# Group-normalised causal attention: key sums by VectorE transposes instead of a TensorE product, and x normalised by ScalarE

## The chip, the cores and the metric

The kernel runs on one core of one Trainium2 chip. The core has five engines that run their own instruction streams: TensorE (PE, matrix products into PSUM), VectorE (DVE), ScalarE (ACT), GpSimd (POOL) and SyncE (SP, which here issues most DMAs). They wait for one another through semaphores. The metric is the time of one execution on the device in microseconds; the times given are medians of several executions.

## The reference, cut to what matters

```
x = x + attention(group_norm(x))          # x: 32 x 256 x 32 x 32, float32

group_norm: 32 groups of 8 channels; (g - mean) / sqrt(var + 1e-5)
xf = normalised x as B x 256 x 1024
q = q_w xf + q_b;   k, v = kv_w xf + kv_b          # 8 heads of 32 channels
scores = q k^T / sqrt(32)                          # 1024 x 1024 per head
mask   = strictly lower triangle                   # a query sees earlier keys only
attn   = softmax(where(mask, scores, -10000)), then 0 where masked
out    = attn v
```

For each batch element: a group normalisation, three projections of 256 x 256, and for each of 8 heads a strictly causal attention over 1024 positions. The softmax needs, for every query, the sum of its exponentials over all keys: the key sum of this document.

## The kernel before

**Layout.** A batch element is x as two tiles of 128 channels by 1024 positions. Four heads of 32 channels share a tile (a channel group `g`), and the 1024 queries are two halves `hf` of 512. Scores are computed transposed: keys lie on the 128 partitions, queries on the free axis. An exponential tile `e` is 128 keys x 4 heads x 512 queries. No maximum is subtracted; the kernel checks at the end that all key sums lay in a safe range and otherwise runs a second path, `shifted()`, which these inputs do not take.

**Visits.** The work of a batch element is cut into N = 12 visits (`visits` and `products`, lines 515 to 526). In visit i, PE makes the scores of one whole tile `e` and one half tile `eh` (`scores`, product at L276), then a part of a projection (`product`, L168), then the value products of the visit before (`values`, L354). ACT turns scores into exponentials (L332 for `e`, two instructions, and L330 for `eh`), POOL zeroes what lies above the diagonal (L290), and DVE adds the tiles of one (group, half) together (L359), so that one tile of 128 x 4 x 512 partial sums is left: `total`, which lives in an `e0` buffer. There are three pairs of PSUM banks for scores, so that the scores of a visit need the exponentials of the visit before to be done. There are three `e`, four `eh` and four `e0` buffers.

**Order.** PE, ACT, DVE and POOL run in the order in which the program text emits instructions (`manual_schedule`). SP's order is found by a scheduler. Two tables say in which visit a piece of work is emitted: `at` (after the visit's scores, ahead of its value products) and `after` (behind its value products). `PROJECT`, `PREPARE`, `SUMS` and `FINISH` (lines 547 to 551) hold the visits, relative to the first visit of the batch.

**Key sums.** For all but the last two batches, each of the four `total` tiles of a batch is folded by two DMAs that add partitions to partitions (`fold`, L372, issued by POOL): from 128 to 64, then to 32 rows. `stack` (L378) copies the 32 rows into a quarter of the tile `folded` (128 partitions: 4 pairs (group, half) x 32 rows, and 4 heads x 512 queries). There is one `folded` buffer. `sum_folded` then sums the 32 rows of each quarter on PE with a matrix of ones in the right places (`pick_half`), four products of 512 columns into the PSUM bank `misc`, and ACT copies the result (`den`, L385) to SBUF. Through two small transfers by way of DRAM (`sums`, then `rows`) the 8192 sums of the batch are spread over 128 partitions x 64. DVE checks their range (L442, L443) and inverts them (L448), the inverses go to DRAM (L450) and come back, repeated over the 32 channels of their head, as four tiles `rb` (L453). `finish` (L466, L467) multiplies the attention output `num` by them and adds the value bias and x. The last two batches (`late`) use `sums` instead, with products by `pick`.

**Normalising.** `norm_channels` takes mean and variance of each channel (L178, L179), `norm_mean` and `norm_variance` average them over 8 channels with small products on PE and copy the results by ACT (L186, L202), `norm_rstd` raises to -0.5 on POOL (L206), and `norm_apply` (L213, DVE) writes the normalised `xn` in four pieces of 128 x 512, one call for each half of the positions. The projections of the next batch begin in visit 7 of the present one and read `xn`.

**The PSUM bank `misc`.** One bank serves the projections, the small products of the norm and the key sum. In visit 6 of each batch, in which the key sum stands at the end, `scores` is given the projection as `between`: ACT's exponentials come in the order first half of `e`, `eh`, second half of `e`, with the projection's copy ahead of the last one.

Of the kernel before, what the change touches and what calls it, by code (L numbers as in the profile page):

```python
# [17 lines left out]
P = 128  # L18
# [13 lines left out]
def tile_norm_attention_residual(  # L32
# [42 lines left out]
    nc.gpsimd.memset(pick, 1.0)  # L75

    pick_half = const.tile([P, 4, CPG], F32, name="pick_half")
    nc.gpsimd.memset(pick_half, 1.0)
    nc.gpsimd.affine_select(
        out=pick_half, in_=pick_half, pattern=[[-HD, 4], [0, CPG]],  # L80
        compare_op=ALU.is_ge, fill=0.0, base=0, channel_multiplier=1,
    )
    nc.gpsimd.affine_select(
        out=pick_half, in_=pick_half, pattern=[[HD, 4], [0, CPG]],
        compare_op=ALU.is_ge, fill=0.0, base=HD - 1, channel_multiplier=-1,
    )
    pick_half = pick_half.rearrange("p a b -> p (a b)")

# [20 lines left out]
    def unshifted():  # L109
# [71 lines left out]
        def norm_mean(b):  # L181
            mv = live["mv", b]
            pm = misc(f"pm_{b}")
            product(pm[:, :NG], avg, mv[:, :, 0])
            mean = small.tile([P, NG], F32, tag="mean", name=f"mean_{b}")
            nc.scalar.copy(mean, pm[:, :NG])  # L186
            live["mean", b] = mean

        def norm_deviation(b):
            mv, mean = live["mv", b], live["mean", b]  # L190

            dev = small.tile([P, NG], F32, tag="dev", name=f"dev_{b}")
            nc.vector.tensor_sub(dev, mv[:, :, 0], mean)
            nc.vector.tensor_mul(dev, dev, dev)
            nc.vector.tensor_add(dev, dev, mv[:, :, 1])
            live["dev", b] = dev
# [8 lines left out]
        def norm_rstd(b):  # L205
            nc.gpsimd.tensor_tensor(live["rstd", b], live["rstd", b], power, ALU.pow)  # L206

        def norm_apply(b, cols):
            if cols.start == 0:
                live["xn", b] = work.tile([P, NG, S], F32, tag="xn", name=f"xn_{b}")  # L210
            mean, rstd = live["mean", b], live["rstd", b]
            for g in range(NG):
                nc.vector.tensor_scalar(  # L213
                    live["xn", b][:, g, cols], live["x", b][:, g, cols],
                    mean[:, g : g + 1], rstd[:, g : g + 1], ALU.subtract, ALU.mult,
                )

# [78 lines left out]

        def scores(b, full, half, between=()):


# [21 lines left out]
            for j in range(2):  # L321
                lo = scores_of((b, half), short[:, j, 0, :], j)
                for ins in first:
                    tc.declare_no_dep(lo.ins, ins.ins, reason="the semaphore orders them")
            for a in (0, 2, 1) if between else (0, 1, 2):
                if a == 1:
                    for f in between:
                        f()
                if a == 2:
                    exp = nc.scalar.activation(eh.rearrange("p (n bank) q -> p bank n q", n=2), short, AF.Exp)  # L330
                else:
                    nc.scalar.activation(e[:, 2 * a : 2 * a + 2, :], pairs[a], AF.Exp)  # L332
# [33 lines left out]


        def fold(b, n, rows):
            total = live["sum", b, *divmod(n, NH)]
            if (n, rows) == (1, HD):  # L370
                nc.gpsimd.drain()
            nc.gpsimd.dma_start(out=total[:rows], in_=total[rows : 2 * rows], accum_op=ALU.add)  # L372
# [6 lines left out]

        def sum_folded(b):  # L380

            pd = misc(f"pd_{b}")
            sum_keys(pd, live.pop(("folded", b)), slice(0, HALF), slice(0, HALF), of_rows=pick_half)
            den = small.tile([P, HALF], F32, tag="den", name=f"den_{b}")
            nc.scalar.copy(den, pd)  # L385
            live["sums", b] = dram.tile([4, 4, HALF], F32, tag="sums", name=f"sums_{b}")
            nc.sync.dma_start(out=live["sums", b].rearrange("j n c -> (j n) c"), in_=den[::CPG, :])

        def sum_keys(pd, e, cols, of, start=True, stop=True, of_rows=pick):
            for j in range(4):  # L390
                nc.tensor.matmul(  # L391
                    pd[HD * j : HD * (j + 1), of], lhsT=of_rows, rhs=e[:, j, cols],
                    start=start, stop=stop, skip_group_check=True,
                )
# [50 lines left out]
        def invert(b, ns):  # L445
            part = slice(ns.start * HD, ns.stop * HD)
            inv = small.tile([P, ROW], F32, tag="inv", name=f"inv_{b}_{ns.start}")
            nc.vector.reciprocal(inv[part], live["rows", b][part])  # L448
            live["inv", b] = dram.tile([4, 4, HALF], F32, tag="inv", name=f"inverses_{b}_{ns.start}")
            nc.sync.dma_start(out=spread_rows(live["inv", b])[part], in_=inv[part])  # L450
            by_half = live["inv", b] if b >= B - 2 else live["inv", b].rearrange("j n c -> n j c")
            for n in ns:
                nc.sync.dma_start(  # L453
                    out=inverses(b, n),
                    in_=by_half[n].unsqueeze(1).broadcast_to([4, HD, HALF]),
                )
# [76 lines left out]
        def prepare(b, whens):  # L533
            both = [slice(hf * HALF, (hf + 1) * HALF) for hf in range(NH)]
            for n, f in zip(whens, (
                lambda: norm_channels(b, 0), lambda: norm_channels(b, 1), lambda: norm_mean(b),
                lambda: norm_deviation(b), lambda: norm_variance(b), lambda: norm_rstd(b),
                lambda: norm_apply(b, both[0]), lambda: norm_apply(b, both[1]),
            )):
                if n is None:  # L540
# [6 lines left out]
        PROJECT = (-5, -4, -3, -2, -1, 0, 1, 2, 3, 4, 5, 6)  # L547
        PREPARE = (-16, -15, -9, -9, -8, -8, -7, -5)
        SUMS = (3, 7, 9, 13)
# [4 lines left out]
        with tc.manual_schedule(engines={ENG.PE, ENG.Activation, ENG.DVE, ENG.Pool}):  # L554
# [19 lines left out]
            for hf in range(NH):  # L574
                norm_apply(0, slice(hf * HALF, (hf + 1) * HALF))
            units = projections(0)
# [5 lines left out]
            if B > 1:  # L582
                prepare(1, (None, None, 0, 1, 2, 3, 3, 3))
            for b in range(B):
# [15 lines left out]
                if not last:  # L600
                    if not late:
                        when(first + N + 6, lambda b=b: sum_folded(b), after)
                    v = first + N + (2 if late else 8)
                    when(v, lambda b=b: gather(b, every))
                    when(v + 2, lambda b=b: check_sums(b, every))
                    when(v + 2, lambda b=b: invert(b, every))
                    for n in every:
# [10 lines left out]
            for i in range(B * N + 1):  # L618
                if i < B * N:

                    between = at.pop(i, ()) if i % N == 6 else ()
                    scores(i // N, *visits[i % N], between)
                for f in at.pop(i, ()):
# [173 lines left out]
```

## Time and profile before

| what | us |
|---|---|
| median of 3 executions (1859.98 to 1860.07) | 1860.05 |
| the profiled execution | 1858.67 |
| its span, first to last instruction | 1856.6 |

| group | count | mean ns | busy us |
|---|---|---|---|
| L332 ACT `e` 128x1024 | 768 | 1022 | 748.0 |
| L330 ACT `eh` 128x1024 | 384 | 1031 | 395.7 |
| L359 DVE adds, four shapes | 762 | | 1153.4 |
| L391 PE key sum of `folded` | 240 | 592 | 31.2 |
| L385 ACT copy `den` | 30 | 586 | 17.6 |
| L213 DVE `xn` 128x512 | 128 | 642 | 76.8 |
| L178 DVE statistics over 128x512 | 128 | 681 | 81.8 |
| L493 DVE reciprocal 128x512 | 1 | 3345 | 3.3 |
| L206 POOL power 128x2 | 32 | 1372 | 43.9 |
| L442, L443, L448 DVE check and inverse | 31 each | 175, 670, 540 | 43.0 |

An engine's busy time is the union of its instructions. PE's matmuls overlap, and each float32 product shows as two instructions, so that four products are eight rows. The profile's chain of waits follows back from the last instruction what released each step. A timeline row has the start, the duration, the engine and line, the operation with its output and inputs, the shape and the count of merged instructions; in square brackets stands how long the engine was idle before, and for whom it waited.

### The profile page before, as it was taken

The numbers are of one execution on the slowest core, as the hardware profiler recorded it, in microseconds if no ns is written. First come the engines' busy times: TensorE is split into PE (matmuls) and PEld (weight loads), VectorE is DVE, ScalarE is ACT, GpSimd is POOL, SyncE is SP. The second block draws the span as 40 slices with busy tenths as digits, with TensorE's granted clock in tenths as the row PEclk, the third lists the DMA queues.
The fourth block names the chain that finished last, engine by engine and source line by source line (L and its number), as shares of the span: only waits on it lengthen the run. The fifth ranks groups of instructions, "written<-read, shape, count | busy, mean of one in ns | idle before, by whom it ended". The sixth has DMA issues, their size and how long they took to land. (4 is left out here: it accounts for less than half of the span.)

```text
span 1856.6 us, 54181 instructions
## 1 busy us (share of the span) xinstructions
PE 1838.8 (99%) x23440; PEld 932.9 (50%) x23440; DVE 1556.5 (84%) x1601; ACT 1414.5 (76%) x1777; POOL 774.5 (42%) x743
## 2 busy tenths in 40 slices
PE   8999999999999999999999999999999999999997
PEld 5454555454554555554545545555455555454543
DVE  4778888888988888888888888888888888888868
ACT  5777777777777777777777777777777777777776
POOL 2543443434434434344344344443443443434314
PEclk9999999999999999999999999999999999999998
DMA  3457665676666676666766666767567666667412
GB/s 120 70 83 144 140 144 114 116 147 139 141 118 127 133 142 140 140 119 122 140 139 143 123 119 131 145 140 145 108 126 145 139 141 114 129 132 141 98 44 89
DMA packets 77517, 233.43 MB, mean 126 GB/s; under 512 B 19808, under 2 KB 20832, under 8 KB 61912
## 3 DMA queue, kind: packets, MB, share of 16 engines
q0 software_dynamic: 15360, 94.39, 36.7%
q1 hardware_dynamic: 61096, 135.51, 24.7%
q8 instruction: 186, 3.05, 0.7%
q14 instruction: 59, 0.48, 0.1%
q10 hardware_dynamic: 816, 0.00, 0.0%
HBM read 68.41 MB, written 35.62 MB: 56 GB/s over the span
## 5 line engine op out<-in xcount | busy, mean ns | idle before, releaser
L332 ACT ACTIVATE e<-sT 128x1024 f32<-128x1024 f32 x768 | 748.0, 1022 | 356.5 <-PE sT L276 302.0
L359 DVE TENSOR_TENSOR e<-e,eh 128x1024 f32<-128x1024 f32 x381 | 524.0, 1389 | 260.4 <-PE acc L354 186.2
L359 DVE TENSOR_TENSOR e<-e,e 128x1536 f32<-128x1536 f32 x381 | 629.4, 1652 | 15.4 <-POOL e L290 1.0
L290 POOL TENSOR_SCALAR_AFFINE_SELECT e<-e 128x512 f32<-128x512 f32 (+1 forms) x256 | 368.3, 1439 | 617.7 <-ACT e L332 595.1
L276 PE MATMUL sT<-q,k 32*128 32x256 f32 (+3 forms) x7168 | 606.3, 458 | 0.8 <-ACT k L230 0.8
L276 PEld LDWEIGHTS sT<-q,k 32*128 32x128 f32 x7168 | 444.1, 184 | 169.9 <-ACT eh L330 65.6
L168 PE MATMUL pp<-xn,wT 128*32 128x512 f32 x4096 | 492.3, 598 | 0.0
L354 PE MATMUL acc<-e,v 128*32 128x512 f32 (+2 forms) x4096 | 400.7, 486 | 0.3 <-POOL e L290 0.3
L330 ACT ACTIVATE eh<-sT 128x1024 f32<-128x1024 f32 x384 | 395.7, 1031 | 0.0
L372 POOL DMA_DIRECT2D e<-e x240 | 199.5, 893 | 400.3 <-PE sT L276 159.7
L168 PE MATMUL ppv<-wT,xn 128*32 128x256 f32 x4096 | 247.3, 382 | 0.0
L354 PEld LDWEIGHTS acc<-e,v 128*32 128x32 f32 x4096 | 132.5, 110 | 223.7 <-issue 200.2
L354 PE MATMUL acc<-eh,v 128*32 128x256 f32 x3072 | 224.4, 379 | 0.0
L168 PEld LDWEIGHTS pp<-xn,wT 128*32 128x32 f32 x4096 | 107.0, 109 | 219.5 <-issue 197.2
L354 PEld LDWEIGHTS acc<-eh,v 128*32 128x32 f32 x3072 | 98.4, 110 | 165.0 <-issue 152.9
L168 PEld LDWEIGHTS ppv<-wT,xn 128*32 128x32 f32 x4096 | 120.2, 109 | 102.5 <-issue 32.1
L290 POOL TENSOR_SCALAR_AFFINE_SELECT eh<-eh 128x512 f32<-128x512 f32 x128 | 165.1, 1289 | 0.1
L230 ACT ACTIVATE k<-pp,qk_bias 128x512 f32<-128x512 f32 x128 | 89.4, 698 | 13.5 <-PE pp L168 12.4
L467 DVE SCALAR_TENSOR_TENSOR rb<-rb,v_bias_col,x 128x512 f32<-128x512 f32 x126 | 95.9, 761 | 4.5
L230 ACT ACTIVATE q<-pp,qk_bias 128x512 f32<-128x512 f32 x128 | 89.9, 702 | 1.9 <-PE pp L168 1.9
L466 DVE TENSOR_TENSOR rb<-num,rb 128x512 f32<-128x512 f32 x126 | 87.8, 696 | 0.1
L178 DVE BATCH_NORM_STATS2 st<-x 128x6 f32<-128x512 f32 x128 | 81.8, 681 | 5.5 <-DMA x<-in_x_dram 5.5
(70 smaller groups left out, 533.1 us busy)
## 6 DMA issues: line engine op xcount, KB each, us to landing
e<-e POOLq DMA_DIRECT2D x120, 512.0 KB, 7.9
x<-in_x_dram SPq DMA_DIRECT2D x64, 512.0 KB
out_dram<-rb SPq DMA_DIRECT2D x127, 256.0 KB
rb<-inverses SPq DMA_DIRECT2D x126, 256.0 KB
e<-e POOLq DMA_DIRECT2D x120, 256.0 KB, 4.6
folded<-e SPq DMA_DIRECT2D x120, 256.0 KB
rows<-sums SPq DMA_DIRECT2D x31, 32.0 KB
inverses<-inv SPq DMA_DIRECT2D x31, 32.0 KB
```

The costliest lines, as they stand in the source:

```text
L168: nc.tensor.matmul(out[part], lhsT=lhsT[:, part], rhs=rhs, start=start, stop=stop, skip_group_check=True)
L178: nc.vector.bn_stats(st[:, c, :], live["x", b][:, g, c * HALF : (c + 1) * HALF])
L230: nc.scalar.activation(live[key][:, cols], pp, AF.Identity, bias=qk_bias[:, n, g : g + 1], scale=(SCALE, 1.0)[n],)
L276: return nc.tensor.matmul(pair[:, cols], lhsT=live["k", b, g][rows, kb * P : (kb + 1) * P], rhs=live["q", b, g][rows, hf * HALF + of.start ...
L290: nc.gpsimd.affine_select(out=diagonal, in_=diagonal, pattern=[[0, 4], [0, n], [1, P]], compare_op=ALU.is_gt, fill=0.0, base=0, channel_mu ...
L330: exp = nc.scalar.activation(eh.rearrange("p (n bank) q -> p bank n q", n=2), short, AF.Exp)
L332: nc.scalar.activation(e[:, 2 * a : 2 * a + 2, :], pairs[a], AF.Exp)
L354: nc.tensor.matmul(acc[HD * j : HD * (j + 1), of], lhsT=live["v", b][:, kb, h * HD : (h + 1) * HD], rhs=e[:, j, cols], start=first, stop=l ...
L359: nc.vector.tensor_add(total[:, :, of], total[:, :, of], e[:, :, cols])
L372: nc.gpsimd.dma_start(out=total[:rows], in_=total[rows : 2 * rows], accum_op=ALU.add)
L466: nc.vector.tensor_mul(rb, num[:, within], rb)
L467: nc.vector.scalar_tensor_tensor(rb, rb, v_bias_col[:, g : g + 1], xt[:, g, cols], ALU.add, ALU.add)
```

## The change

For all but the last two batches, `sum_folded` no longer uses PE. For each of the four heads DVE turns the 128 x 512 slice of `folded` in square blocks of 32 x 32 (`transpose`), so that the 32 rows of a quarter come to lie along the free axis, and adds them up along it (`tensor_reduce`) into 16 columns of `rows`. Two heads are done behind visit 6, two behind visit 7. `rows` is thus filled on the chip, with no copy by ACT and no `sums` and `rows` transfers. Check and inversion move from visit N+10 to N+8. The inverses are turned back by one more transpose of 128 x 64 and written to DRAM by four DMAs, in runs of 32 values. `pick_half` goes. The last two batches keep their way of summing and its visits.

`norm_apply` handles one of four pieces of 128 x 512 per call, behind visits 5, 6, 7 and 8, and is an ACT instruction, rstd * x + shift, with shift = -mean * rstd from a new small product on POOL; batch 0 stays with DVE. ACT writes the mean with its sign turned. `between` goes, and with it the special order of exponentials in visit 6.

```diff
         def norm_mean(b):
...
-            nc.scalar.copy(mean, pm[:, :NG])
-            live["mean", b] = mean
+            nc.scalar.activation(mean, pm[:, :NG], AF.Identity, scale=-1.0)
+            live["minus_mean", b] = mean
...
         def norm_rstd(b):
-            nc.gpsimd.tensor_tensor(live["rstd", b], live["rstd", b], power, ALU.pow)
+            rstd = live["rstd", b]
+            nc.gpsimd.tensor_tensor(rstd, rstd, power, ALU.pow)
+            live["shift", b] = small.tile([P, NG], F32, tag="shift", name=f"shift_{b}")
+            nc.gpsimd.tensor_tensor(live["shift", b], live["minus_mean", b], rstd, ALU.mult)
...
+        def norm_apply(b, hf, g):
...
+            cols = slice(hf * HALF, (hf + 1) * HALF)
+            xn, xt = live["xn", b][:, g, cols], live["x", b][:, g, cols]
+            rstd = live["rstd", b][:, g : g + 1]
+            if b == 0:
+                nc.vector.tensor_scalar(xn, xt, live["minus_mean", b][:, g : g + 1], rstd, ALU.add, ALU.mult)
+            else:
+                nc.scalar.activation(xn, xt, AF.Identity, bias=live["shift", b][:, g : g + 1], scale=rstd)
...
-            for a in (0, 2, 1) if between else (0, 1, 2):
-                if a == 1:
-                    for f in between:
-                        f()
+            for a in range(3):
...
-        def sum_folded(b):
-
-            pd = misc(f"pd_{b}")
-            sum_keys(pd, live.pop(("folded", b)), slice(0, HALF), slice(0, HALF), of_rows=pick_half)
-            den = small.tile([P, HALF], F32, tag="den", name=f"den_{b}")
-            nc.scalar.copy(den, pd)
-            live["sums", b] = dram.tile([4, 4, HALF], F32, tag="sums", name=f"sums_{b}")
-            nc.sync.dma_start(out=live["sums", b].rearrange("j n c -> (j n) c"), in_=den[::CPG, :])
+        def sum_folded(b, heads):
+            if heads.start == 0:
+                live["rows", b] = small.tile([P, ROW], F32, tag="rows", name=f"rows_{b}")
+            for j in heads:
+                turned = small.tile([P, HALF], F32, tag="den", name=f"turned_{b}_{j}")
+                nc.vector.transpose(turned, live["folded", b][:, j, :])
+                nc.vector.tensor_reduce(
+                    live["rows", b][:, j * HALF // HD : (j + 1) * HALF // HD],
+                    turned.rearrange("p (k r) -> p k r", r=HD), AX.X, ALU.add,
+                )
...
-            nc.sync.dma_start(out=spread_rows(live["inv", b])[part], in_=inv[part])
...
+            if b >= B - 2:
+                nc.sync.dma_start(out=spread_rows(live["inv", b])[part], in_=inv[part])
+            else:
+                turned = small.tile([P, ROW], F32, tag="inv_turned", name=f"inv_turned_{b}")
+                nc.vector.transpose(turned, inv)
+                for n in ns:
+                    nc.sync.dma_start(
+                        out=live["inv", b][n].rearrange("(a j) (m c) -> (j m) a c", a=2, c=HD),
+                        in_=turned[n * HD : (n + 1) * HD].rearrange("p (a c) -> p a c", a=2),
+                    )
...
-        PREPARE = (-16, -15, -9, -9, -8, -8, -7, -5)
+        PREPARE = (-16, -15, -9, -9, -8, -8, -7, -6, -5, -4)
...
-                    if not late:
-                        when(first + N + 6, lambda b=b: sum_folded(b), after)
-                    v = first + N + (2 if late else 8)
-                    when(v, lambda b=b: gather(b, every))
-                    when(v + 2, lambda b=b: check_sums(b, every))
-                    when(v + 2, lambda b=b: invert(b, every))
+                    if late:
+                        when(first + N + 2, lambda b=b: gather(b, every))
+                    else:
+                        when(first + N + 6, lambda b=b: sum_folded(b, every[:2]), after)
+                        when(first + N + 7, lambda b=b: sum_folded(b, every[2:]), after)
+                    v = first + N + (4 if late else 8)
+                    when(v, lambda b=b: check_sums(b, every))
+                    when(v, lambda b=b: invert(b, every))
```

## The prediction

> **What bounds the kernel now.** I read the page's first two parts, then the waits of TensorE (PE), then the timeline around one visit in the middle, and last the chain. One batch is twelve visits. Batch 15 is used throughout; its visit 6 begins at 901.11 us of the span.
>
> ```profile
> PE 1838.8 (99%) x23440; PEld 932.9 (50%) x23440; DVE 1556.5 (84%) x1601; ACT 1414.5 (76%) x1777; POOL 774.5 (42%) x743
> PEclk9999999999999999999999999999999999999998
> ```
>
> PE is busy 99% in every slice at a full granted clock. A busy share alone proves little, since the ends of matmuls are modelled, so the starts decide:
>
> ```profile
> 901.11 1.57 PE L276 MATMUL sT<-q,k 32*128 32x256 f32 x16
> ...
> 905.21 0.61 PE L354 MATMUL acc<-eh,v 128*32 128x256 f32 x8
> 905.64 1.04 PE L391 MATMUL pd<-folded,pick_half 128*32 128x512 f32 x8
> 906.62 1.58 PE L276 MATMUL sT<-q,k 32*128 32x256 f32 x24
> ...
> 911.27 1.57 PE L276 MATMUL sT<-q,k 32*128 32x256 f32 x16
> ...
> 929.89 1.57 PE L276 MATMUL sT<-q,k 32*128 32x256 f32 x16
> ...
> 934.54 1.58 PE L276 MATMUL sT<-q,k 32*128 32x256 f32 x24
> ```
>
> The L276 rows are the score products with which a visit begins. Visit 6 lasts 906.62 - 901.11 = 5.51 us. Visit 0 (929.89 to 934.54) has the same tile shapes and lasts 4.65; visit 7, 4.65 as well. The only thing more in visit 6 is the key sum at L391, so that costs PE 0.86 us. In PE's waits all causes add up to about 9 us, at the program's two ends. In the stretch 897.00 to 953.85 (one batch, 56.85 us) PE is busy all 56.85, DVE 48.45 and ACT 43.92. So PE sets the pace, and DVE and ACT have some 8 and 13 us to spare per batch. The chain agrees in the middle; only its last 50 us run over DVE.
>
> **PE: what goes.** L391 with `folded` stands for 240 instructions, 8 a time, so 30 batches. 30 x 0.86 = 25.8 us, if nothing else becomes late. `pick_half`'s setup on POOL (0.24 + 0.22 + 0.12 us) goes too, beside the first load (DVE waits 5.16 us for it): nothing.
>
> **ACT: four applies in, one copy out.** Per batch `den` (0.59) goes and four `xn` of 128x512 come. These are the rows to price one by:
>
> ```profile
> L230 ACT ACTIVATE q<-pp,qk_bias 128x512 f32<-128x512 f32 x128 | 89.9, 702 | 1.9 <-PE pp L168 1.9
> L362 ACT COPY num<-acc 128x512 f32<-128x512 f32 x128 | 76.4, 597 | 8.9 <-PE acc L354 8.9
> ```
>
> L230 carries one per-partition operand (the bias), L362 none. The nearest row alone would say 0.70 us, and the only row out of SBUF (L479, two of them) 0.72. The Trainium skill, "ScalarE: Activation LUTs", section "What ACT_TABLE_LOAD costs", says that each per-partition pointer operand adds about 93 ns and that instructions in a row overlap by as much. The two rows differ by 105 ns, which agrees, and the apply has two pointers (scale and bias): 0.70 + 0.10 = 0.80. By the row four applies are 2.8 us, by the rule 3.2; I take 0.80, or 0.70 net of overlap. ACT becomes 43.92 - 0.59 + 3.2 = 46.5 of 56.0 us. What counts is the place. The applies follow the projection's copy (and `num`, where there is one) and stand ahead of the next visit's first exponential, for which ACT now idles:
>
> ```profile
> 902.29 1.02 ACT L332 ACTIVATE e<-sT 128x1024 f32<-128x1024 f32 x1 [0.94 <-PE sT L276]
> ...
> 906.75 0.59 ACT L385 COPY den<-pd 128x512 f32<-128x512 f32 x1
> 908.09 1.94 ACT L332 ACTIVATE e<-sT 128x1024 f32<-128x1024 f32 x2 [0.75 <-PE sT L276]
> ...
> 912.46 1.94 ACT L332 ACTIVATE e<-sT 128x1024 f32<-128x1024 f32 x2 [0.94 <-PE sT L276]
> ...
> 916.74 1.94 ACT L332 ACTIVATE e<-sT 128x1024 f32<-128x1024 f32 x2 [0.37 <-PE sT L276]
> ```
>
> The number in brackets is idle time. Visits 6 and 8 have 0.94 for 0.70: hidden. In visit 7 the apply takes `den`'s place: `num` still starts 0.14 us into the visit, ends at 0.73, the apply at about 1.43, and the exponential is due at 1.47: hidden with next to nothing over. In visit 9, 0.37 is too little: its exponentials come 0.33 later. There `eh` ends at 919.59, PE wants that bank at 920.57, so 0.98 - 0.33 = 0.65 us is left: still hidden. At the end of visit 7, 0.33 us remain too (`eh` ends at 910.94, products at 911.27). So an apply stalls PE only from about 1.1 us on. The new order of exponentials in visit 6 (whole tile first, `eh` last) lets `eh` end 4.04 us into it, as in visit 0, before 4.65: nothing.
>
> PE also waits for the applies. The first projection from `xn` comes in visit 7 and needs the first two: the second channel group, ready at about 1.43, is read only by the second half of the products (1.51 + 0.86 = 2.37). The next pair, for visit 9, has the same margin of some 0.8 us.
>
> **POOL: one small multiply.** It stands behind the power at L206 (896.93 to 898.37); behind it is a mask at 900.00, for which POOL idled 1.63 us. Its price lies between L295 (0.10) and the power itself (1.44); both fit, and the first apply is not due before 901.25. Taken as 0.3, hidden. Mean by an ACTIVATE with a factor instead of a copy: at most L202 - L186 = 0.10 us, once on the start-up path.
>
> **DVE: four applies out, transposes and sums in.** Out: 4 x 0.642 (L213) = 2.57. In: per batch four transposes T and four reductions R of 128x512, one transpose of 128x64. R: nearest is L178, which also reads 512 columns into a few, 0.68. The Trainium skill, "VectorE: DVE Perf Modes", "Rules for kernel authors", speaks against this: a reduction on a hot path is the slowest vector operation and should be restructured. By that rule the change would give PE's gain back; by the row, four R are 2.7 us on an engine that has 8 to spare, so the rule doesn't decide here. T has no row: not below half of L213's quickest pair (1.00 us at 912.27), 0.5, and not above the dearest DVE row at this size, the reciprocal L493, 3.35. I take 0.70, the price of L178, an operation that passes each element once. Sum: 4 x (0.70 + 0.68) + 0.15 - 2.57 = +3.1, DVE 51.6 of 56.0 us.
>
> The place again: between 903.42 and the add at 919.90 DVE idles twice, 1.94 and 2.79 us = 4.73. There come 5.5 (sums) + 1.55 (checks, reciprocal, transpose, two visits earlier than now) and go 2.42 (applies): +4.6, in a stretch 0.86 shorter. So DVE arrives about 0.8 us late at 919.90, and catches up in visit 10, which no longer has the checks (1.4). Who waits for DVE: exponentials, for a free `e` or `eh`. The nearest is `eh` of visit 11 (928.53), which needs the add that ends at 921.1: 7 us of cover.
>
> **Queues.** SP loses the stores of `sums` and `inverses` and the load of `rows`, and gets four small stores: one issue more per batch (0.3 to 0.5 us). The next batch's first `stack` now waits for DVE's fourth transpose instead of PE's sum; behind it queue only the inverse stores, which need DVE later still. The inversion moves up two visits and past the second `stack`, which then waits behind four stores, their landing (now 70.4 us in 32 waits, 2.2 each) and four broadcasts; that tile is read some 30 us later. The first output is multiplied at 940.11; broadcasts are issued from 928.03 now and then some 6 us earlier: hidden even if stores in 128-byte runs land 2 us slower. The two transfers through DRAM that go were hidden already.
>
> **Sum.** The profiled execution took 1858.67 us around its span of 1856.6. 1858.67 - 25.8 + 0.1 (start) + 0.1 (the last but one batch, where an apply and a `den` copy meet) = 1833.1. The median shown is 1.4 us above the profiled one, so the forecast is **1834.5 us**.
>
> **Rivals.**
> - *ACT becomes late* (chance 0.09). For: visits 7 and 8 end with 0.33 and less to spare. Against: it needs applies of over 1.1 us, or other gaps. At 1.3 us visits 7 and 8 lose some 0.2 each: 30 x 0.4 = 12, so 1846.
> - *DVE becomes the bound, slower than before* (0.05). Mechanism: a transpose of 4-byte elements that runs at a quarter of the rate, like the 128x2048 add of L359 (2.27 us). DVE would need 48.45 - 2.57 + 0.15 + 4 x (2.27 + 0.68) = 57.8 us a batch: 30 x (57.8 - 56.85) = +29, so 1888. It decides from T = 2.0 on. Against: one pass over 512 columns is 0.7.
> - *The 0.86 us turn into another wait* (0.02): the key sum gave ACT time to copy in visit 6, and PE waits for the bank instead. Time 1860. Against: without `den` ACT has less to do there, and the sums above leave a gap.
>
> The forecast has 0.84. Its own range is 1833 to 1837. Half of the ACT case and the small margin in visit 7 extend it to 1841; the low end is 1832.5, since only PE's 25.8 us are there to win. A measurement of this kernel tells about 0.2% (3.7 us) from no change. Faster 0.93 (forecast and ACT case), same 0.02, slower 0.05.
>
> **What would show it.** Visit 6 at 4.65 us from start to start, PE's waits near 9 us, applies at about 0.80 us on ACT, the idle time before the exponentials of visit 9 gone, T + R near 1.4 and DVE near 92%. It is wrong if exponentials wait for DVE's adds, if PE waits for `eh` or `xn`, or if T is over 2 us.

## The result, and the profile after

The median went from 1860.06 us (1859.98 to 1860.38, 4 runs) to 1836.63 us (1836.06 to 1837.18, 4 runs): a ratio of 0.9874, with a 95% interval of 0.9859 to 0.9889. That is 23.4 us less; the forecast was 25.6 less (1834.5). The same two kernels measured later on another chip (`after_again`, below) came to 1861.32 and 1836.78, 24.5 less. The profiled execution of the changed kernel took 1836.99 us, its span 1835.3. The lines below are of this kernel, so their numbers have shifted: scores L269, exponentials L321 and L319, value products L343, adds L348.

The timeline of PE around visit 6 of batch 15 (start, duration, engine and line, operation, tiles, shape, count):

```profile
891.17 1.57 PE L269 MATMUL sT<-q,k 32*128 32x256 f32 x16
892.68 1.92 PE L156 MATMUL pp<-xn,wT 128*32 128x512 f32 x16
894.42 1.05 PE L343 MATMUL acc<-e,v 128*32 128x384 f32 x16
895.28 0.61 PE L343 MATMUL acc<-eh,v 128*32 128x256 f32 x8
895.83 1.58 PE L269 MATMUL sT<-q,k 32*128 32x256 f32 x24
```

The score products of visit 7 follow directly on the last value product: 895.83 - 891.17 = 4.66 us where there were 5.51. The other visits of batch 15 have kept their length to the hundredth (0: 4.65, 2: 4.22, 3: 5.12, 9: 5.08), so this batch takes 55.99 us instead of 56.85. Thirty visits 6 make 30 x 0.86 = 25.8.

The groups that are new, by shape (count, busy us and mean ns of one, then the idle time before them):

```profile
L209 ACT ACTIVATE xn<-x,shift,rstd 128x512 f32<-128x512 f32 x124 | 103.3, 833 | 0.0
...
L375 DVE STREAM_TRANSPOSE turned<-folded 128x512 f32<-128x512 f32 x120 | 84.2, 702 | 0.0
L376 DVE TENSOR_REDUCE rows<-turned 128x16 f32<-128x512 f32 x120 | 82.3, 686 | 4.1
...
L197 POOL TENSOR_TENSOR shift<-mean,rstd 128x2 f32<-128x2 f32 x32 | 22.3, 695 | 2.5
...
L446 DVE STREAM_TRANSPOSE inv_turned<-inv 128x64 f32<-128x64 f32 x30 | 7.4, 245 | 1.0
```

And batch 15 as one stretch (length, then busy us and instructions of PE, weight loads, DVE, ACT and POOL, then the granted clock):

```profile
863.12:919.11 55.99, 55.99 (x725) 28.60 (x722) 51.95 (x56) 46.06 (x59) 25.10 (x25) 1.00 0.67 133
```

PE still fills the batch. DVE has gone from 48.45 to 51.95 us in this batch and ACT from 43.92 to 46.06. Over the page, PE is at 99%, DVE at 90% (84% before) and ACT at 81%.

**Where 2.4 us of the 25.8 stayed.** From the start of the first visit to the start of the last, the profiled execution went from 1819.06 to 1795.08 us: 24.0 less. The rest of the gain is missing in three places, for which the prediction had only 0.1. Visit 3 of two batches is 0.27 and 0.34 us longer, because in visit 2 an exponential waits for the second `stack` of the batch before to free its `e0` buffer. In the last batch but one (visits 8 and 9, counted from the start of batch 30) 1.15 us are missing. Both waits stand in the groups and waits of ACT:

```profile
ACT e L321 <- DMA folded<-e: 16.1, 12, 1.9
```

```profile
L416 ACT COPY den<-pd 128x512 f32<-128x512 f32 x6 | 3.5, 586 | 7.7 <-PE pd L383 5.4 <-DVE rows L376 2.2
```

In the first, the numbers are the sum, the times and the longest in us: twelve waits, nearly all hidden. In the second, one copy of the late way of summing waits 2.2 us for a reduction of the new way: `turned` was put under the tag `den`, which has two buffers, so the two ways share them. This wait is about 1.0 of the 1.15 us: where it is taken away (experiment 7), 0.16 us remain, and `norm_only`, which has the applies on ACT but no `turned`, has 0.19 more in visit 9 as well.

The other differences between the two profiled executions can't be put down to moving the key sum. The first score product of the changed kernel starts at 18.28 us instead of 16.74, and what follows the start of the last visit is 1.1 us longer. But a run with the key sum still on PE (`norm_only`, below) starts its scores at 17.84 us and has the same end of 22 us, and all other profiled runs lie between 17.84 and 19.17: the kernel before was the odd one in its profiled execution, which at 1858.67 lay below its own median. Of the 1.1 us at the end, 0.9 are one short instruction of DVE, which is told in the last section. In these two traces the start goes with the granted clock; the stretches from 11 to 13 us, of before and of after:

```profile
11.00:13.00 2.00, 2.00 (x20) 1.42 (x22) 1.63 (x4) 1.35 (x3) 0.33 (x1) 1.00 1.02 410
```

```profile
11.00:13.00 2.00, 2.00 (x12) 2.00 (x11) 1.67 (x4) 1.39 (x3) 0.49 (x2) 0.50 1.03 414
```

PE was granted its full clock in the first and half in the second, and the same twelve transposes of weights take 1.53 us before and 2.69 after. The cause stays open: in `sums_only` and `turn_reduce_twice` they take 2.82 us, though the profile shows no half clock there.

### The profile page after: what moved, and what is told of

It reads as the page before. It is cut to its first block, busy times and chain, and to the rows that moved or that the text cites. A ratio compares the mean times of both kernels' runs of the same rounds, so it can differ in the third digit from the quotient of the medians.

```text
span 1835.3 us, 53874 instructions
## 1 busy us (share of the span) xinstructions
PE 1815.7 (99%) x23200; PEld 925.6 (50%) x23200; DVE 1650.8 (90%) x1747; ACT 1481.1 (81%) x1871; POOL 797.1 (43%) x772
## 4 chain that ended last, share of the span: by engine, by line
PE 96%; DVE 3%; ACT 1%; issue 0%; DMA 0%; SPq 0%; DVEq 0%; ACTq 0%
PE sT L269 31%; PE acc L343 26%; PE pp L156 25%; PE ppv L156 13%; DVE e L348 1%; DVE rb L493 0%; DVE rb L466 0%; ACT e L321 0%; DMA x<-in_x_dram 0%; DVE rb L467 0%; PE pv L156 0%; ACT eh L319 0%; PE pd L383 0%; PE wt L135 0%; PE pm L156 0%
## 5 line engine op out<-in xcount | busy, mean ns | idle before, releaser
L321 ACT ACTIVATE e<-sT 128x1024 f32<-128x1024 f32 x768 | 745.9, 1025 | 274.6 <-PE sT L269 202.5
L348 DVE TENSOR_TENSOR e<-e,e 128x1536 f32<-128x1536 f32 x381 | 638.8, 1677 | 20.3 <-POOL e L283 2.7
L348 DVE TENSOR_TENSOR e<-e,eh 128x1024 f32<-128x1024 f32 x381 | 523.9, 1389 | 133.6 <-PE acc L343 113.6
L283 POOL TENSOR_SCALAR_AFFINE_SELECT e<-e 128x512 f32<-128x512 f32 (+1 forms) x256 | 379.4, 1482 | 591.6 <-ACT e L321 571.6
L269 PE MATMUL sT<-q,k 32*128 32x256 f32 (+3 forms) x7168 | 607.2, 458 | 0.8 <-ACT k L223 0.8
L269 PEld LDWEIGHTS sT<-q,k 32*128 32x128 f32 x7168 | 443.0, 184 | 158.0 <-ACT eh L319 65.6
L343 PE MATMUL acc<-e,v 128*32 128x512 f32 (+2 forms) x4096 | 400.7, 486 | 0.0
L319 ACT ACTIVATE eh<-sT 128x1024 f32<-128x1024 f32 x384 | 397.6, 1036 | 0.0
L343 PEld LDWEIGHTS acc<-e,v 128*32 128x32 f32 x4096 | 132.5, 110 | 223.4 <-issue 192.1
L343 PE MATMUL acc<-eh,v 128*32 128x256 f32 x3072 | 224.4, 379 | 0.0
L343 PEld LDWEIGHTS acc<-eh,v 128*32 128x32 f32 x3072 | 98.4, 110 | 165.0 <-issue 152.9
L209 ACT ACTIVATE xn<-x,shift,rstd 128x512 f32<-128x512 f32 x124 | 103.3, 833 | 0.0
```

What stands on the lines that cost most here:

```text
L209: nc.scalar.activation(xn, xt, AF.Identity, bias=live["shift", b][:, g : g + 1], scale=rstd)
L269: return nc.tensor.matmul(pair[:, cols], lhsT=live["k", b, g][rows, kb * P : (kb + 1) * P], rhs=live["q", b, g][rows, hf * HALF + of.start ...
L283: nc.gpsimd.affine_select(out=diagonal, in_=diagonal, pattern=[[0, 4], [0, n], [1, P]], compare_op=ALU.is_gt, fill=0.0, base=0, channel_mu ...
L343: nc.tensor.matmul(acc[HD * j : HD * (j + 1), of], lhsT=live["v", b][:, kb, h * HD : (h + 1) * HD], rhs=e[:, j, cols], start=first, stop=l ...
L348: nc.vector.tensor_add(total[:, :, of], total[:, :, of], e[:, :, cols])
```

## The experiments

Averages of visits are over batches 5 to 24. Two theories about the gain stood against each other: that PE's key sum is all of it, and that part of it comes from moving the normalisation. About the limit there were two as well: that DVE has some 4 us a batch to spare, as its busy time says, or that it is nearer to being the bound.

**1. `norm_only`: only the normalisation moves.** The kernel before, with the four applies on ACT, the shift on POOL and the new `PREPARE`; the key sum stays on PE.

```diff
-                nc.vector.tensor_scalar(
-                    live["xn", b][:, g, cols], live["x", b][:, g, cols],
-                    mean[:, g : g + 1], rstd[:, g : g + 1], ALU.subtract, ALU.mult,
-                )
...
+                nc.scalar.activation(xn, xt, AF.Identity, bias=live["shift", b][:, g : g + 1], scale=rstd)
...
-        PREPARE = (-16, -15, -9, -9, -8, -8, -7, -5)
+        PREPARE = (-16, -15, -9, -9, -8, -8, -7, -6, -5, -4)
```

> The kernel before with only the x normalisation moved to ScalarE in four pieces; the key sums stay on PE with their special order in visit 6. Theory (all of the gain is PE's key sum): 1860 (1859 to 1861.5), visit 6 still 5.51 us, VectorE some 2.6 us a batch less busy for nothing. Rival (relief of VectorE is part of the gain): 1850 or less. Rival (the pieces cost time on ScalarE): 1865 or more.

Measured: 1861.47 us against 1860.40 (ratio 1.0007, 0.9998 to 1.0015). The timeline of PE around its visit 6:

```profile
902.20 1.57 PE L281 MATMUL sT<-q,k 32*128 32x256 f32 x16
...
906.73 1.04 PE L396 MATMUL pd<-folded,pick_half 128*32 128x512 f32 x8
907.71 1.58 PE L281 MATMUL sT<-q,k 32*128 32x256 f32 x24
```

The key sum is there and the visit lasts 5.51 us. So moving the normalisation alone gains nothing, and the four applies on ACT cost PE nothing.

**2. `sums_only`: only the key sums move.** The changed kernel, with `norm_apply` back on DVE, two pieces behind visit 5 and two behind visit 7.

```diff
-                nc.scalar.activation(xn, xt, AF.Identity, bias=live["shift", b][:, g : g + 1], scale=rstd)
+            nc.vector.tensor_scalar(xn, xt, live["minus_mean", b][:, g : g + 1], rstd, ALU.add, ALU.mult)
...
-        PREPARE = (-16, -15, -9, -9, -8, -8, -7, -6, -5, -4)
+        PREPARE = (-16, -15, -9, -9, -8, -8, -7, -7, -5, -5)
```

> The key sums by VectorE as in the changed kernel, but x normalised by VectorE as before (two pieces behind visit 5, two behind visit 7; the latter stand behind the transposes and sums of visit 7). Theory (PE sets the pace, and what counts for VectorE is the place of each piece, not its share): VectorE needs about 54.3 of 56.0 us a batch, which would fit, but the second pair of x pieces comes about 2.4 us into visit 9, where PE wants it at 1.5: PE waits about 1 us a batch for it, 30 batches, so about 1866 (1860 to 1870), and PE's waits show VectorE's x pieces. Rival (only the share counts): 1837, no such wait. Rival (VectorE is then the bound outright): well above 1870, with exponentials waiting for VectorE's adds.

Measured: 1874.19 us, slower than before (1.0075, 1.0058 to 1.0092) and above the 1860 to 1870 of the theory: the place of the loss was right, the size too small. Among PE's waits:

```profile
PE pp L156 <- DVE xn L204: 26.1, 28, 1.3
```

Visit 6 is 4.65 us here too, but visit 9 is 6.07 instead of 5.08, where PE waits for `xn`, and visit 3 is 0.31 longer. The gain of visit 6 is given back in other visits of the same batch.

**3. `sums_early`: the same, with all four applies behind visit 5.** It was to take the wait for `xn` away.

```diff
-        PREPARE = (-16, -15, -9, -9, -8, -8, -7, -7, -5, -5)
+        PREPARE = (-16, -15, -9, -9, -8, -8, -7, -7, -7, -7)
```

> As sums_only, but all four x pieces on VectorE stand behind visit 5, ahead of the transposes. Theory (place, not share): the same load on VectorE, x is ready about 5 us into visit 6 and wanted 6.1 us into it, so PE waits for nothing: 1837 to 1840. Rival (VectorE's share of some 97% of a batch is too much wherever it stands): about as slow as sums_only, 1860 and more.

Measured: 1915.27 us (1.0294, 1.0276 to 1.0312): a miss by far. Visit 9 is 5.08 again, as meant, but visit 2 rose from 4.22 to 5.22 and visit 3 from 5.12 to 6.90. The waits of PE and of ACT show the way:

```profile
PE sT L264 <- ACT e L316: 32.1, 50, 2.3
```

```profile
ACT e L316 <- DMA folded<-e: 104.3, 27, 5.4
```

The likely chain: DVE, held up by the applies, finishes the inverses later; their stores and the broadcasts stand on SP ahead of the batch's second `stack`; an `e0` buffer comes free only when that `stack` has read it; ACT wants the buffer in visit 2 of the next batch. Only its last link is in the lines above; experiment 7 tests the queue, in the changed kernel. The wait moved from one visit to two others.

**4. `reduce_twice`, `turn_reduce_twice`: DVE loaded further.** In the changed kernel each reduction is done twice (4 x 0.686 = +2.7 us a batch), then each transpose too (+5.5). The values are the same.

```diff
                 nc.vector.transpose(turned, live["folded", b][:, j, :])
+                nc.vector.transpose(turned, live["folded", b][:, j, :])      (second kernel only)
+                nc.vector.tensor_reduce(
...
                 nc.vector.tensor_reduce(
...
```

> Each sum along rows by VectorE is done twice (the second overwrites the first with the same values): 4 x 0.69 = 2.75 us more a batch on VectorE, 51.95 + 2.75 = 54.7 of 56.0. Theory (VectorE is off the path until about 56 us): within 3 us of the changed kernel, 1837 to 1840. Rival (at 90% busy VectorE is the bound already): 30 x 2.75 = 82 more, about 1919.

> Each transpose and each sum along rows is done twice: 5.55 us more a batch on VectorE, 57.5 against 56.0 us. Theory (VectorE becomes the bound from 56.0 on): 30 x (57.5 - 56.0) = 45 us more and, with the waits that VectorE can't avoid (2.3 us a batch now), up to 110 more: 1880 to 1945, exponentials waiting for VectorE's adds. Rival (some other slack hides it): 1840 or less.

Measured: 1888.53 us (1.0157, 1.0140 to 1.0174) and 1971.88 us (1.0605, 1.0588 to 1.0623). The first is a miss, the second costs more than the top of what was expected. In `reduce_twice` the loss lies in visit 4 (6.48 instead of 4.75), where PE's small product `pv` waits for the three short deviation instructions:

```profile
908.78 0.24 PE L156 MATMUL pv<-dev,avg 128*32 128x2 f32 x8 [1.69 <-DVE dev L183]
```

This is a waiter that the prediction did not name. Two readings were left: that this wait is the one thin spot, or that DVE as a whole has become the bound and `pv` only happens to be the first in line.

**5. `reduce_twice_dev_early`, `reduce_twice_all_mended`: the thin spot taken away.** Both have the doubled reductions. The mean and the deviation are emitted behind visit 1 instead of 3; the second kernel has the repairs of experiment 7 too.

```diff
-        PREPARE = (-16, -15, -9, -9, -8, -8, -7, -6, -5, -4)
+        PREPARE = (-16, -15, -11, -11, -8, -8, -7, -6, -5, -4)
```

> The doubled reductions again (VectorE +2.75 us a batch), but the mean and the three small deviation instructions are emitted behind visit 1 instead of visit 3, so that two visits lie between them and the small product pv that PE makes in visit 4. Theory: the 28 us a batch sum lost with doubled reductions were PE waiting in visit 4 for the deviation, and nothing else; then visit 4 is 4.75 again, PE no longer waits on that line, and the time is 1837 to 1845 (some single visits 3 longer, by the late second stack). Rival: VectorE as a whole is too late and only the next waiter in the order takes the wait over (exponentials of visit 2, visit 3 then 5.5 to 6.5): 1860 to 1889.

> The same, with the broadcasts also moved behind visit 11 and the turned tile in its own buffer. Theory: with both known ways from VectorE to PE opened, VectorE at some 54.7 of 56.0 us a batch costs PE nothing: visits 3 and 4 at 5.12 and 4.75 in all batches, 1835.5 to 1840. Rival: a third waiter, not named yet, keeps the time above 1850.

Measured: 1921.29 us (1.0329, 1.0311 to 1.0346) and 1928.54 us (1.0372, 1.0355 to 1.0390). Visit 4 is 4.93 and PE no longer waits for `dev`, but both times are worse than that of `reduce_twice`, and the first lies above even its rival's 1860 to 1889. The theory of one thin spot falls. New waits have come up. PE's own in the steady batches are for POOL's masks, for its fill of one row and for ACT's copies (18.8, 15.5 and 7.9 us), not for DVE; ACT's in `reduce_twice_dev_early` are:

```profile
ACT num L351 <- DVE rb L470: 48.9, 25, 3.6
ACT e L321 <- DVE e L348: 38.9, 13, 3.1
...
ACT eh L319 <- DVE e L348: 28.5, 26, 1.2
```

They are all waits for DVE: for the outputs, before a `num` buffer comes free, and for the adds, before an `e` or `eh` buffer does. What all these kernels have in common is found by splitting the batch on DVE itself, from the start and end of each of its instructions, averaged over twenty batches (5 to 24). "Waits" are gaps of over 0.15 us, "gaps" the shorter ones between instructions, which stay (some 1.9 us) even where DVE never waits. The three columns add up to the batch.

| kernel | batch us | DVE busy | gaps | waits | busy with L348's adds |
|---|---|---|---|---|---|
| before | 56.85 | 48.79 | 1.38 | 6.67 | 36.55 |
| `norm_only` | 56.85 | 46.69 | 1.58 | 8.57 | 36.54 |
| after | 56.01 | 51.95 | 1.69 | 2.36 | 36.84 |
| `sums_only` | 57.29 | 55.17 | 1.57 | 0.54 | 37.01 |
| `sums_early` | 58.82 | 56.49 | 1.62 | 0.63 | 37.90 |
| `reduce_twice` | 57.80 | 55.91 | 1.88 | 0.00 | 38.04 |
| `reduce_twice_dev_early` | 58.98 | 57.07 | 1.95 | 0.05 | 39.13 |
| `reduce_twice_all_mended` | 59.44 | 57.38 | 2.02 | 0.05 | 39.01 |
| `turn_reduce_twice` | 60.61 | 58.62 | 2.03 | 0.02 | 38.32 |

(The adds are L359 before the change; the line differs by kernel.) The changed kernel leaves DVE 2.36 us a batch, not 4. Doubled reductions ask for 2.75, and then DVE never waits again: it is the bound, and where PE meets it is a matter of the order. The sum closes: busy +3.96, of which 2.75 are the second reductions and 1.20 the adds, which have become longer; idle -2.17; together +1.79, the measured 57.80 - 56.01. Why the adds get longer is told in the last section. Those of `turn_reduce_twice` are 1.48 us a batch longer than in the changed kernel, some 44 us over 30 batches, which its expected range did not have. That moving `dev` made it worse still is explained in part only: the adds grew by another 1.09 us a batch, because they start with more of POOL's masks still to run (last section), but why this order brings that about was not tried.

The table also says more of experiments 2 and 3 than their own waits do. The key sums ask for 4 x (0.702 + 0.686) + 0.245 = 5.8 us, and without the move of the normalisation a batch of 55.99 leaves just 6.67 - 0.86 = 5.8 of waits. Busy time and gaps of `sums_only` come to 56.7 us, those of `sums_early` to 58.1: neither fits into 55.99. The waits for `xn` and for the `e0` buffer are where PE met a DVE that was all but full.

**6. `apply_twice`: ACT loaded further.** Each apply is done twice (+2.9 us of ACT a batch, beside 9.9 idle).

```diff
                 nc.scalar.activation(xn, xt, AF.Identity, bias=live["shift", b][:, g : g + 1], scale=rstd)
+                nc.scalar.activation(xn, xt, AF.Identity, bias=live["shift", b][:, g : g + 1], scale=rstd)
```

> Each x piece on ScalarE is written twice: 4 x 0.73 = 2.9 us more a batch, 46.06 + 2.9 = 49 of 56.0 us. Theory (place counts: an x piece of more than about 1.1 us makes the exponentials of visits 7 and 8 so late that PE waits for the bank): PE loses some 0.35 us at the end of visit 7, 0.5 at visit 8 and 0.2 at visit 9, 31 batches: about 1868 (1855 to 1880), although ScalarE's share is only 88%. Rival (share counts): 1837.

Measured: 1883.51 us (1.0128, 1.0111 to 1.0145); slower, as the theory said, but above its 1855 to 1880, and the places are not those named. Visits 7, 8 and 9 were to lose 0.35, 0.5 and 0.2 us; they take +0.17, +0.00 and +1.34. PE in visit 9:

```profile
925.17 2.21 PE L270 MATMUL sT<-q,k 32*128 32x256 f32 x16
927.31 1.07 PE L156 MATMUL pp<-xn,wT 128*32 128x512 f32 x8
928.87 1.07 PE L156 MATMUL pp<-xn,wT 128*32 128x512 f32 x8 [0.49 <-ACT xn L210]
```

The score products take 2.21 us instead of 1.57, held by the exponentials of visit 8, and the projection waits 0.49 us for the last piece of `xn`. ACT runs from 911.6 to 932 without a wait, four visits in a row, and the lateness adds up; at 83% of the span it is still far from full. So ACT's room is local too: one apply a visit fits, two don't.

**7. `own_buffer`, `late_spread`, `both_mended`: the 1.8 us that were lost.** The first gives `turned` a buffer of its own; the second issues the broadcasts of the inverses behind visit 11, so that the second `stack` stands behind one of them instead of four; the third does both. `after_again` is the changed kernel, for comparison on the same chip.

```diff
-                turned = small.tile([P, HALF], F32, tag="den", name=f"turned_{b}_{j}")
+                turned = small.tile([P, HALF], F32, tag="turned", bufs=1, name=f"turned_{b}_{j}")
...
+            if b >= B - 2:
+                spread(b, ns)
+
+        def spread(b, ns):
             for n in ns:
                 nc.sync.dma_start(
...
+                    if not late:
+                        when(first + N + 11, lambda b=b: spread(b, every), after)
```

> The changed kernel itself, to be compared with the next three on the same chip: about 1836.6 by every theory.

> The changed kernel with one buffer of its own for the turned slices, instead of the two that they share with ScalarE's copies of key sums in the last two batches. Theory (in the last but one batch ScalarE's copy waited 2.18 us for VectorE's sum to free that buffer, and PE lost 1.15 us in visits 8 and 9): 1.2 us less than after_again, that wait gone. Rival (the copy would have waited for PE anyway): no difference.

> The changed kernel with the four broadcasts of the inverses issued behind visit 11, so that the second stack of the next batch stands on the queue behind one broadcast instead of four. Theory (the stack was late because of the broadcasts, and an exponential tile of visit 2 waits for the buffer that it frees): ScalarE's waits for that transfer, 16.1 us in 12 times, go to nearly none, and with them PE's 0.6 us in two batches: 0.6 less than after_again. Rival (the stack waits for the fold ahead of it, not for the broadcasts): the waits stay.

> Both of the last two edits together. Theory: 1.8 us less than after_again, about 1834.8, and 1.3% less than before. Rival: no difference.

| kernel | median us | lowest, highest | start of first to start of last visit |
|---|---|---|---|
| `after_again` | 1836.78 | 1836.12, 1837.22 | 1795.12 |
| `own_buffer` | 1837.01 | 1835.90, 1838.14 | 1794.20 |
| `late_spread` | 1836.35 | 1836.20, 1837.33 | 1794.45 |
| `both_mended` | 1835.39 | 1835.14, 1836.64 | 1793.45 |

In `late_spread` visit 3 is 5.12 in every steady batch, and ACT has no wait for `folded` left. In `own_buffer` and `both_mended` the 2.2 us wait of the `den` copy is gone; in `both_mended` the last batch but one takes 60.07 us instead of 61.06. So both losses are shown by their own waits. The times of the single repairs can't be told from `after_again` (their runs overlap, and `own_buffer`'s median, expected to be 1.2 us lower, is not). Both together are 1.4 us lower at the median, where 1.8 were expected; these runs overlap too, by one of four, and the firmer number is the 1.7 us between the visits in the profiles. `both_mended` is the fastest of all, at a ratio of 0.9865 (0.9849 to 0.9882) to before, an interval that overlaps with the change's.

## Why the prediction was right

**PE.** The step "the only thing more in visit 6 is the key sum at L391, so that costs PE 0.86 us" held to the hundredth, and `norm_only` shows that it is the whole gain. Of the three rivals none came: PE's waits are some 11 us in all, none in the middle of the program, where 9 were named; 1.2 of the difference are at the very end (last section). One reading was too strong: the page's digits show 90% or more of a slice, not 99% in every one, but the forecast rests on the starts of visits.

**ACT.** By the nearest row an apply would take 0.70 us, by what the Trainium skill, "ScalarE: Activation LUTs", section "What ACT_TABLE_LOAD costs", says of pointer operands 0.80; it took 0.83, nearer to the rule. ACT's batch is 46.06 against 46.5: four applies added 46.06 - 43.92 + 0.59 = 2.73, or 0.68 each net of overlap, for which 0.70 stood in the prediction but not in its sum. The timeline of ACT in visits 7 to 9, which begin at 895.83, 900.48 and 904.70:

```profile
896.45 0.81 ACT L209 ACTIVATE xn<-x,shift,rstd 128x512 f32<-128x512 f32 x1
897.30 1.94 ACT L321 ACTIVATE e<-sT 128x1024 f32<-128x1024 f32 x2
...
901.67 1.94 ACT L321 ACTIVATE e<-sT 128x1024 f32<-128x1024 f32 x2 [0.24 <-PE sT L269]
...
905.44 0.85 ACT L209 ACTIVATE xn<-x,shift,rstd 128x512 f32<-128x512 f32 x1
906.15 1.97 ACT L321 ACTIVATE e<-sT 128x1024 f32<-128x1024 f32 x2
```

In visit 7 the apply ends 897.26 - 895.83 = 1.43 us into the visit, as worked out, and the exponential starts at 1.47. In visit 8 there is 0.24 to spare. In visit 9 the idle time is gone and the exponentials start at 1.45 us, some 0.2 late (0.33 was reckoned) and hidden. The point at which it would stall, 1.1 us an apply, was bounded only: 1.65 us in `apply_twice` stalls.

**POOL.** The multiply took 0.70 us, between the ends of 0.10 and 1.44 but over the 0.3 that was taken; hidden: in `norm_only`, which has it too, every steady visit keeps its length.

**DVE.** T was taken as 0.70 and measured 0.702; R as 0.68, measured 0.686; the small transpose 0.245 for 0.15. T had no row of its own and was priced by likeness with L178, so that it came out to the hundredth is in part luck. The Trainium skill, "VectorE: DVE Perf Modes", section "Rules for kernel authors", calls a reduction the slowest vector operation; here it costs what other passes over 512 columns cost (0.702 for a transpose, 0.69 for an add alone), and the measurement decides. The sum was 51.6, measured 51.95. What was low is the base: batch 15, which the prediction read, is the one of batches 5 to 24 that needs only 48.45. The next batch, like nearly all others, needs 48.8:

```profile
929.89:986.74 56.85, 56.85 (x733) 28.85 (x729) 48.80 (x51) 43.93 (x56) 24.34 (x24) 1.00 0.66 132
```

So the step itself was +3.15 where +3.1 was forecast. The place came true as well: the add that was to be some 0.8 us late starts 5.25 us into visit 9 instead of 4.40, and the first one of visit 10, 3.88 instead of 4.33 us into it, has caught up.

What the prediction had too generous is the room. It set busy time against the batch, "on an engine that has 8 to spare"; the table gives 6.67 us of waits before and 2.36 after, since 1.4 to 1.7 us of a batch are short gaps. The rival "DVE becomes the bound" was to decide "from T = 2.0 on". By the table DVE stops having waits at 2.36 / 4 = 0.59 us more for each head, so from about T = 1.3; and `reduce_twice`, with 0.69 more, is already slower than before. T was well below, so the forecast stood, but with less cover than it claimed.

**The queues.** The clause "that tile is read some 30 us later" named the wrong reader. The second `stack` also frees the `e0` buffer that it reads, and that is wanted in visit 2 of the next batch. It cost 0.6 us in the changed kernel and is the wait in which `sums_early` lost its time. The shared tag `den`, which cost about 1 us once, was in the diff and was overlooked: the 0.1 that the prediction had for the last batch but one, where an apply and a `den` copy meet, is the other 0.16.

**The sum.** 1834.5 was forecast as the median and 1836.63 measured. 0.6 and about 1.0 of the 2.1 us are these two waits; the rest is within the spread of the runs. That waits nobody had reckoned with stayed at 1.6 us, inside the range of 1833 to 1837, is luck: of the first kind ACT had 16.1 us in the changed kernel, nearly all hidden, and 104.3 in `sums_early`.

## What to carry to other kernels

Work taken off the bounding engine is gained in full only while the engine that receives it keeps true waits: count its idle gaps by length, and set the added time against the long ones, not against one minus the busy share. Here one half of the change made room for the other: moving the key sums alone lost 0.75%, moving the normalisation alone nothing, both together won 1.3%. For every buffer that a moved step reads, ask who wants the buffer next, and not only who wants its result; and give a new temporary a tag of its own where an older way of working still uses the old one.

## What was not expected of the hardware

**An add of two tensors on DVE that starts while POOL masks takes longer; transposes and reductions don't.** The timelines of DVE and of POOL in the changed kernel over the same stretch:

```profile
896.90 1.51 DVE L348 TENSOR_TENSOR e<-e,eh 128x1024 f32<-128x1024 f32 x1
...
899.67 0.70 DVE L375 STREAM_TRANSPOSE turned<-folded 128x512 f32<-128x512 f32 x1
900.41 0.69 DVE L376 TENSOR_REDUCE rows<-turned 128x16 f32<-128x512 f32 x1
901.01 1.22 DVE L348 TENSOR_TENSOR e<-e,eh 128x1024 f32<-128x1024 f32 x1
```

```profile
896.36 0.97 POOL L283 TENSOR_SCALAR_AFFINE_SELECT eh<-eh 128x512 f32<-128x512 f32 x1
899.31 1.10 POOL L283 TENSOR_SCALAR_AFFINE_SELECT e<-e 128x1024 f32<-128x1024 f32 x1 [1.98 <-ACT e L321]
```

The add that starts inside a mask takes 1.51 us, the one with no mask beside it 1.22; the transpose at 899.67, wholly inside a mask, takes its 0.70. Over the steady batches an add of 128x1024 takes 1.22 us alone and mostly 1.51 or 1.94 when it starts inside a mask, one of 128x512 takes 0.69 or 1.05, and the transposes and reductions are the same in both cases to 0.01. This agrees with the Trainium skill, "SBUF — State Buffer", section "Who interferes with whom": a vector instruction with two SBUF inputs contends with a GpSimd instruction that reads SBUF, and a reduction doesn't.

The size follows from the traces. The first add above starts 0.43 us before the end of its mask and is 0.29 us longer. The 201 adds of the steady batches that start inside a mask have on average 0.46 us of it ahead of them and are 0.34 longer; in `reduce_twice` it is 199 adds, 0.60 and 0.47; in `reduce_twice_dev_early` 208 adds, 0.66 and 0.53. So an add loses what is left of the mask, less some 0.13 us. This is why the last column of the table grows: a full DVE starts no more of its adds inside masks, but starts them with more of the mask to come.

Of the 1.1 us by which the end of the program is longer, 0.9 are the same effect. Before, a check of 128 x 1 ran just ahead of a mask; in all other profiled kernels it started inside that mask. Before and after:

```profile
1840.13 0.16 DVE L489 SCALAR_TENSOR_TENSOR in_range<-most,least 128x1 f32<-128x1 f32 x1
```

```profile
1817.69 1.05 DVE L489 SCALAR_TENSOR_TENSOR in_range<-most,least 128x1 f32<-128x1 f32 x1
```

**Half the clock behind a pause of PE.** In `reduce_twice`, behind the wait at `pv` in batch 15, by stretch (the granted clock is third from the end):

```profile
910.00:911.00 1.00, 1.00 (x16) 0.68 (x16) 0.96 (x2) 0.50 (x1) 1.00 (x1) 0.55 1.13 244
911.00:913.00 2.00, 2.00 (x12) 0.39 (x8) 1.90 (x2) 2.00 (x3) 1.56 (x3) 0.50 0.81 252
```

PE had paused 1.7 us, until 908.78. From about 910 to 913.5 it was granted half its clock, and visit 5 took 6.30 us instead of 4.66. In that kernel it happened once, though the pause is 1.3 to 1.7 us in 26 batches. In `turn_reduce_twice` the pause is longer:

```profile
PE pv L156 <- DVE dev L183: 66.5, 28, 2.7
```

There visit 5 takes 6.0 to 6.3 us in 15 of these 28 batches. In the steady batches of `apply_twice` (pauses of 0.5 us) and `sums_only` (up to 1.3) it never happens. So the pauses very likely bring it on; what decides which of them do was not tried. `reduce_twice` lost nothing by it: batches 15 and 16 took 59.47 + 55.99 = 115.46 us, no more than two others (2 x 57.82), since DVE was the bound.
